# A four-layer graph network: attention sums in chunks of 32 edge tiles with a PSUM place for each tile, and four smaller edits

## The chip, the cores and the metric

The kernel runs on one core of one Trainium2 chip, in one launch. The metric is device time in microseconds (us), the median of several runs. A separate profiled execution gives the rows that are quoted here; it has its own time, which is given beside the median below. Engines are named as in the profile: PE (TensorE, with PEld for its weight loads), DVE (VectorE), ACT (ScalarE), POOL (GpSimd) and SP (SyncE), which here mostly issues DMAs.

## The reference

There are N = 6250 nodes with 128 features and E = 100000 edges sorted by their destination. The node features pass through four layers. After each of them stands `x = layernorm(x + layer(x))`.

- Layer 0 is graph attention, two sublayers: `g = h @ W`, one score per edge `e = leaky_relu(s[src] + d[dst])`, a softmax over the edges that share a destination, and `out = segment_sum(g[src] * alpha)`. A loop edge per node is included.
- Layer 1 is a graph convolution: `out = segment_sum(xw[row] * dis[row] * w * dis[col])`.
- Layer 2 is attention with eight heads. Per edge it has a relation embedding (64 types), a sigmoid time mask from `timestamps[dst] - edge_time`, a gate from a small network, then query of the destination, key and value of the message, softmax over the destination's edges, and a sum.
- Layer 3 sums `m[src]` over each destination's edges and feeds the sum to a GRU cell.

All of it is in float32. Each layer so has the same heart: rows of a node table are fetched for the sources of all edges, something is done per edge, and the results are summed per destination.

## The kernel before

**Edge tiles and blocks.** The nodes are 49 blocks of P = 128. The edges are packed into K = 832 tiles of 128 edges, each of which belongs to one block of destinations. A tile is summed by one matmul: its one-hot matrix `sel` (edge by node, f32, 128 x 128) is the stationary operand, the tile's 128 rows the moving one, and the product is what the tile adds to its block. `ACC` in SBUF holds the sums of all blocks, W = 136 columns each.

**Gathers.** `gather` (L137) is an indirect DMA on POOL's queue: 128 rows of a table in DRAM, one per partition. One stage has 832 of them. They fill row tiles `g` of U = 16 edge tiles.

**One-hot matrices.** `selections` (L365) gives `sel` for 16 tiles. In the first attention sublayer DVE makes it (L372) and SP stores it to `SELD`; later stages load it by SP (L370, 1 MB). `row_selections` (L377) gives the transposed one-hot `rsel` in bf16, which takes node values to edges. In the first sublayer it is made from a broadcast row of destination numbers (`dlrow`, L385) by a comparison on DVE (L386), and stored (L387); later it is loaded (L389).

**Sums.** The class `Windows` (L402) sums tiles in groups (L445) through a ring of PSUM banks. A bank is a window of 3 tiles (4 in `sum_edges`). The tiles of a window belong to neighbouring blocks, often to the same one, so a window has places for blocks relative to its first block: PE loads each tile's place into a register (L415, called in L434), the window is set to zero by a small matmul (L437, 1 x 128 by 1 x 408 or 512), and the tiles' matmuls accumulate at their places. DVE then adds the whole window to `ACC` (L453), at the register offset of the window's first block. Before the add of a chunk's first window, L451 fades what is in `ACC`, because the softmax reference of a block that goes on from the previous chunk may have changed.

**Attention.** `attention_edges` (L460) runs for l0 and l1. It takes the tiles in chunks, `CHUNKS = [48] * 17 + [16]`. Per chunk it loads flags (L483 on, SP), gathers the rows into `g` (7 buffers of 16 tiles), and forms the destination's value of each edge by small matmuls of `rsel` with values split into three bf16 terms (L493 into `pd`; in l0 also the node times, L496 into `pn`; the two lie in one bank, `pdn`). Then comes the softmax reference of the chunk, a chain between DVE and PE with transposes and scans (L499 to L547: `de`, `e`, `fw`, `tot`, `car`, `back`, `cin`, `ref`, `f`, `fac`). Then ACT takes the exponentials (L550) and scales each tile's rows (L556), and `sums.add` takes the tiles. The instructions of one chunk's sums and of the next chunk's chain stand between each other on the engines. The values for `rsel`'s matmuls come from `by_step` (L349), which makes one three-term table per value: `D0` for each sublayer, `NV` for the node times.

**The other edge stages.** `sum_edges` (L561) serves the graph convolution (c, with a scaling on ACT, L575) and the last layer (m, without): 8 buffers of `g`, windows of 4 tiles, two windows a group. Layer 2's table stage writes queries, `Qt`, split into three bf16 terms (L787 to L791). Its edge loop goes in 208 steps of B = 4 tiles: `rows_of` (L817) issues the gathers `xa`, the query loads `qb` (one per tile, at a register's offset, SP), the `rsel` loads and others; `keys` has for each tile one matmul for key and value (`pk`, L890) and three bf16 matmuls that bring the query to the edges (`pq`, L892). The values are stored to DRAM. The softmax reference (xw) follows, with flags loaded by SP (L1003), and then the sum (vw), which uses `Windows` with 3 tiles and 4 windows a group.

**What orders the work.** Within an engine instructions run in the order written out by the program's planner; across engines semaphores order them. `first_after(x, names)` (L392) makes `x` wait for the named instructions; `in_order` only keeps an order on one engine. A tile with n buffers makes its next use wait for the last reader n uses back: so POOL waits for PE, when it is as many row tiles ahead as there are buffers. DMAs of one engine's queue are issued in order.

Of the kernel before, what the change touches and what calls it, by code (L numbers as in the profile page):

```python
# [9 lines left out]
F32 = mybir.dt.float32  # L10
# [10 lines left out]
P = 128  # L21
NB = 49
# [17 lines left out]
CHUNKS = [48] * 17 + [16]  # L40
T = max(CHUNKS)
HD = 8
# [8 lines left out]
def kernel(ctx: ExitStack, tc: tile.TileContext, a: dict, out: bass.AP):  # L51
# [5 lines left out]
    def table(name, rows, width, dtype=F32):  # L57
        return dram.tile([rows, width], dtype, name=name)
# [20 lines left out]
    RSELD = table("rseld", K // U * P, U * P, BF16)  # L79
    TYR = table("tyr", KR, P, BF16)  # L80
# [5 lines left out]
    Qt = table("qt", NP, 3 * W, BF16)  # L86
# [30 lines left out]
    OFF = const.tile([97, K + 4], I32, name="OFF")  # L117
    PLACE = {3: OFF[0:1, 0:K], 4: OFF[64:65, 0:K]}
    QOFF = OFF[32:33, 0:K]
    FIRST = {3: OFF[96:97, 0:K // 3 + 1], 4: OFF[96:97, K // 3 + 1:K // 3 + 1 + K // 4]}  # L120
# [22 lines left out]
    with tc.tile_pool(name="prep", bufs=1) as pp, tc.tile_pool(name="prepp", bufs=2, space=PSUM) as pq:  # L143
# [97 lines left out]
        for m, w in WINDOWS.items():  # L241
            n = -(-K // m)
            part = 0 if m == 3 else 64
            steps = bkrow[part:part + 1, 0:n * m].rearrange("o (w s) -> o w s", s=m)
            place = pp.tile([P, K + 4], F32, name="place", bufs=2)[part:part + 1, 0:n * m]
            nc.vector.tensor_sub(place.rearrange("o (w s) -> o w s", s=m), steps,
                                 steps[:, :, 0:1].to_broadcast([1, n, m]))
            nc.vector.tensor_scalar(PLACE[m], place[:, 0:K], float(w), None, op0=OP.mult)
            nc.vector.tensor_scalar(FIRST[m], bkrow[96:97, 0:n * m:m], float(W), None, op0=OP.mult)
        nc.vector.tensor_scalar(QOFF, bkrow[32:33, 0:K], float(P), None, op0=OP.mult)  # L250

# [97 lines left out]
    def by_step(keep, work, psum, rows, name):  # L349


        v = work.tile([P, K], F32, name="bsv", bufs=1)
        for k0 in range(0, K, K // 2):
            pv = psum.tile([P, K // 2], F32, name="bs", bufs=1)
            nc.tensor.matmul(pv, rows, BSEL[0:NB, k0:k0 + K // 2], start=True, stop=True)
            nc.vector.tensor_copy(v[:, k0:k0 + K // 2], pv)
        t3 = keep.tile([P, K, 3], BF16, name=f"{name}t", bufs=1)
        for i in range(3):
            nc.vector.tensor_copy(t3[:, :, i], v)
            if i < 2:  # L360
                nc.vector.tensor_sub(v, v, t3[:, :, i])
        return t3
# [14 lines left out]
    def row_selections(work, k0, make=False, n=U):  # L377

        rs = work.tile([P, n * P], BF16, name="rsel", bufs=4 if n < U else 2)
        tab = RSELD[k0 // U * P:(k0 // U + 1) * P, k0 % U * P:(k0 % U + n) * P]  # L380
        if make:
            for h in range(2):
                n = U * P // 2
                row = work.tile([P, n], BF16, name="dlrow")
                nc.sync.dma_start(row, flat(DLR, k0 * P + h * n, (0, P), (1, n)))  # L385
                nc.vector.tensor_scalar(rs[:, h * n:(h + 1) * n], row, relid, None, op0=OP.is_equal)  # L386
            last = nc.sync.dma_start(tab, rs)  # L387
        else:
            last = nc.sync.dma_start(rs, tab)  # L389
        return rs, name_of(last)  # L390
# [10 lines left out]

    class Windows:  # L402
# [4 lines left out]
        def __init__(self, psum, m, banks, windows):  # L407
            self.m, self.w, self.banks, self.group = m, WINDOWS[m], banks, windows * m
            self.ring = psum.tile([P, banks, BANK], F32, name="ring")
            self.todo = []  # L410
            for t0 in range(0, NB + MW, 14):
                nc.vector.memset(ACC[:, t0:min(NB + MW, t0 + 14), :], 0.0)
# [7 lines left out]
        def add(self, k, sel, rows, after, fade=None, kept=0):  # L420

# [5 lines left out]
            if fade is not None:  # L427
                self.fades[k] = fade
# [18 lines left out]
            for v in wins:  # L447
                to = self.to[v % U]
                if v * m in self.fades:
                    a0 = ACCF[:, ds(to, kept)]  # L450
                    nc.vector.tensor_scalar(a0, a0, self.fades.pop(v * m), None, op0=OP.mult)  # L451
                a0 = ACCF[:, ds(to, m * W)].rearrange("p (b w) -> p b w", w=W)[:, :, 0:n]
                add = nc.vector.tensor_add(a0, a0, self.ring[:, v % self.banks, 0:m * w]  # L453
                                           .rearrange("p (b w) -> p b w", w=w)[:, :, 0:n])
                if v == wins[0]:
                    first_after(add, name_of(last))

        fades = {}

    def attention_edges(l, D3, NV3):  # L460
        extra = 1 if l == 0 else 0
        with ExitStack() as es:
            work = es.enter_context(tc.tile_pool(name=f"aw{l}", bufs=2))
            rows = es.enter_context(tc.tile_pool(name=f"ar{l}", bufs=7))
            psum = es.enter_context(tc.tile_pool(name=f"ap{l}", bufs=1, space=PSUM))
            sums = Windows(psum, 3, 6, 2)
# [6 lines left out]
            pd, pn = (pdn[:, i * 3 * T:(i + 1) * 3 * T].rearrange("p (t i) -> p t i", i=3) for i in range(2))  # L473
# [4 lines left out]
            for T_ in CHUNKS:  # L478
                gs = []
                flags = work.tile([T, 4, P], BF16, name="flags")[0:T_]  # L480
# [5 lines left out]
                for u0 in range(0, T_, U):  # L486
                    g = rows.tile([P, U, GW + 3], F32, name="g")
                    gs.append((g, [gather(g[:, q, 0:GW], Gt[l], SRCT[:, k0 + u0 + q:k0 + u0 + q + 1])
                                   for q in range(U)]))
                    rs, _ = row_selections(work, k0 + u0, l == 0)  # L490
                    for q in range(U):
                        k = k0 + u0 + q
                        nc.tensor.matmul(pd[:, u0 + q, :], rs[:, q * P:(q + 1) * P], D3[:, k, :],  # L493
                                         start=True, stop=True)
                        if l == 0:
                            nc.tensor.matmul(pn[:, u0 + q, :], rs[:, q * P:(q + 1) * P], NV3[:, k, :],  # L496
                                             start=True, stop=True)
                if l == 0:
                    nc.vector.tensor_reduce(TMT[:, k0:k0 + T_], pn[:, 0:T_, :], AX.X, OP.add)  # L499
                de = work.tile([P, T], F32, name="de")[:, 0:T_]  # L500
                nc.vector.tensor_reduce(de, pd[:, 0:T_, :], AX.X, OP.add)
# [59 lines left out]
    def sum_edges(name, src_tab, weighted):  # L561

        with ExitStack() as es:
# [3 lines left out]
            sums = Windows(psum, 4, 8, 2)  # L567
            for k0 in range(0, K, U):
                g = rows.tile([P, U, D], F32, name="g")
                got = [gather(g[:, q, :], src_tab, SRCT[:, k0 + q:k0 + q + 1]) for q in range(U)]  # L570
                sel, made_by = selections(work, k0)
                for q in range(U):
                    after = name_of(got[q])
                    if weighted:
                        scaled = nc.scalar.activation(g[:, q, :], g[:, q, :], AF.Copy,  # L575
                                                      scale=EWT[:, k0 + q:k0 + q + 1])
                        after += name_of(scaled)
                    sums.add(k0 + q, sel[:, q, :], g[:, q, :], made_by + after)

# [71 lines left out]
    with tc.tile_pool(name="l0", bufs=1) as lp:  # L651
        SD = [lp.tile([P, 2, NB], F32, name=f"SD{l}") for l in range(2)]
        D3 = [None, None]
        with tc.tile_pool(name="n0w", bufs=2) as work, tc.tile_pool(name="n0p", bufs=1, space=PSUM) as psum:
# [11 lines left out]
            NV3 = by_step(lp, work, psum, nv, "NV")  # L666
            D3[0] = by_step(lp, work, psum, node_rows(work, psum, SD[0][:, 1, :]), "D0")
        attention_edges(0, D3[0], NV3)
        with tc.tile_pool(name="n1w", bufs=2) as work, tc.tile_pool(name="n1p", bufs=1, space=PSUM) as psum:
# [6 lines left out]
            D3[1] = by_step(lp, work, psum, node_rows(work, psum, SD[1][:, 1, :]), "D0")  # L676
        attention_edges(1, D3[1], None)
# [47 lines left out]
    with tc.tile_pool(name="l2", bufs=1) as lp:  # L725
# [26 lines left out]
        with tc.tile_pool(name="n3w", bufs=2) as work, tc.tile_pool(name="n3p", bufs=1, space=PSUM) as psum:  # L752
# [21 lines left out]
            for t0, g in GROUPS:  # L774
# [5 lines left out]
                q3 = work.tile([P, B, 3, W], BF16, name="q3")  # L780
# [6 lines left out]
                for i in range(3):  # L787
                    nc.scalar.copy(q3[:, :g, i, :], qt[:, :g])
                    if i < 2:
                        nc.vector.tensor_sub(qt[:, :g], qt[:, :g], q3[:, :g, i, :])  # L790
                nc.sync.dma_start(nodes(Qt)[:, t0:t0 + g, :], q3[:, :g].rearrange("p t i w -> p t (i w)"))  # L791
# [5 lines left out]
        with ExitStack() as es0:  # L797
# [7 lines left out]
            with ExitStack() as es:  # L805
# [11 lines left out]
                def rows_of(n):  # L817
# [4 lines left out]
                    qb = rows.tile([P, B, 3, W], BF16, name="qb", bufs=4)  # L822
# [3 lines left out]
                    loads = [nc.sync.dma_start(qb[:, q].rearrange("p i w -> p (i w)"), Qt[ds(vals[q], P), :])  # L826
# [3 lines left out]
                    rs = row_selections(work, k0, n=B)  # L830
                    landed[n] = [i.ins.name for i in loads] + rs[1]
                    rs = rs[0]
# [45 lines left out]
                def keys(n, mT, qb, rs):  # L878
# [6 lines left out]
                    for q0 in range(0, B, 2):  # L885
                        pk = pks[:, q0 // 2]
                        pq_ = pqs[:, q0 // 2, 0:2 * W].rearrange("p (q w) -> p q w", w=W)
                        for q in range(q0, q0 + 2):
                            o = q * P
                            part(nc.tensor.matmul(pk[:, q - q0, :], mT[:, q, :], Wkv, start=True, stop=True), after)  # L890
                            for i in range(3):
                                part(nc.tensor.matmul(pq_[:, q - q0, :], rs[:, o:o + P], qb[:, q, i, :],  # L892
                                                      start=i == 0, stop=i == 2), after)
# [62 lines left out]
            with tc.tile_pool(name="xw", bufs=1) as work, tc.tile_pool(name="xp", bufs=1, space=PSUM) as psum:  # L956
# [40 lines left out]
                for g0 in range(0, NG, 4):  # L997
                    pr = psum.tile([P, 4, P], F32, name="prr", bufs=2)
                    for i in range(4):
                        tot = TOT[:, g0 + i, :]  # L1000
                        fl = work.tile([P, 2, P], BF16, name="fl", bufs=4)
                        for way in range(2):
                            flags_of(2 + way, fl[:, way, :], g0 + i, nc.sync)  # L1003
# [217 lines left out]
```

## Time and profile before

| | us |
|---|---|
| median of 3 runs | 8168.42 (8152.12 to 8171.95) |
| profiled execution, its time | 8259.27 |
| profiled execution, its span | 8257.5 |

The profiled span, by stage:

| stage | from | to | what |
|---|---|---|---|
| l0 | 146 | 1700 | attention, first sublayer |
| l1 | 1757 | 3213 | attention, second sublayer |
| c | 3345 | 4540 | weighted sum |
| tables | 4634 | 4687 | queries and other node tables of layer 2 |
| L2 loop | 4687 | 6410 | messages, keys, values, scores |
| xw | 6410 | 6512 | softmax reference of layer 2 |
| vw | 6512 | 6822 | sum of layer 2 |
| m | 6914 | 8133 | plain sum |

Over the span PE is busy 47%, DVE 32%, ACT 21%, POOL 51%. The profile's rows read as follows. In a row of the waits: engine, line and tile that waited, then the releaser, the sum in us, how often, and the longest. "issue" is time in which the engine waited for nothing that the profile shows, "remote" a releaser that it cannot name. In a row of the timeline: start and length in us, engine, line, operation, written tile and read tiles, shape, how many in a row, and in brackets the idle time before it with its releaser. The granted clock is TensorE's, as a share of full speed.

### The profile page before, as it was taken

To read this page: it belongs to the slowest core of one execution; us is meant where nothing else is said; L and a number is where in the kernel's file an instruction comes from. 1 tells how busy PE (TensorE), PEld (TensorE's weight loads), DVE (VectorE), ACT (ScalarE), POOL (GpSimd) and SP (SyncE) were. 2 spreads that over 40 slices of the span, in tenths; PEclk is the share of its full clock that TensorE was granted. 3 is DMA by queue.
4 is the path that set the end of the run, shared out by engine and by line. 5 is a ranking of instruction groups with operands and counts; after the bars stand their busy time and mean duration, and the time that the engine had idled before them with its cause. 6 is when DMAs were issued, how large, how long until landed. Compare 5 with 4: busy or idle time off the path is not lost. (4 is left out here: it accounts for less than half of the span.)

```text
span 8257.5 us, 75556 instructions
## 1 busy us (share of the span) xinstructions
PE 3922.3 (47%) x20491; PEld 2792.2 (34%) x20491; DVE 2618.2 (32%) x5807; ACT 1708.1 (21%) x5176; POOL 4221.7 (51%) x4384
## 2 busy tenths in 40 slices
PE   2244444433334433233333377777777693243436
PEld 1133333322223322222222244444444472132224
DVE  3122222231111114110111666566566654011115
ACT  1112121202211111222222233333333110000001
POOL 2555555435555551656666155455553373666661
PEclk8555555555555555555555688788888796555657
DMA  4333433333333322222332466666666592232321
GB/s 109 93 118 111 120 111 118 94 91 108 96 96 96 98 79 59 78 88 88 96 92 89 133 184 186 179 187 185 181 185 169 193 360 66 70 97 87 98 88 60
DMA packets 737110, 997.93 MB, mean 121 GB/s; under 512 B 151865, under 2 KB 594033, under 8 KB 703425
## 3 DMA queue, kind: packets, MB, share of 16 engines
q1 hardware_dynamic: 588090, 662.03, 25.4%
q0 software_dynamic: 146992, 331.03, 16.2%
q8 instruction: 189, 3.10, 0.2%
q14 instruction: 217, 1.77, 0.1%
q10 hardware_dynamic: 1622, 0.01, 0.0%
HBM read 824.55 MB, written 168.09 MB: 120 GB/s over the span
## 5 line engine op out<-in xcount | busy, mean ns | idle before, releaser
L445 PE MATMUL ring<-g,sel 128*128 128x128 f32 (+2 forms) x6656 | 1532.7, 388 | 1755.5 <-issue 1723.6
L137 POOL DMA_INDIRECT g<-g,SRCT x1664 | 1573.0, 945 | 1524.8 <-issue 836.9
L445 PEld LDWEIGHTS ring<-g,sel 128*128 128x128 f32 x6656 | 1336.8, 288 | 2119.7 <-issue 2119.6
L453 DVE TENSOR_TENSOR ACC<-ACC,ring 128x512 f32 (+3 forms) x1250 | 755.9, 605 | 3734.0 <-remote 2206.2
L137 POOL DMA_INDIRECT xa<-xat,SRCT x832 | 855.4, 1028 | 970.0 <-DVE z L872 582.5
L137 POOL DMA_INDIRECT g<-yt,SRCT x832 | 785.0, 943 | 589.8 <-issue 394.7
L137 POOL DMA_INDIRECT g<-mt,SRCT x832 | 785.0, 944 | 489.6 <-issue 345.5
L437 PE MATMUL ring<-zero 1*128 1x408 bf16 (+1 forms) x1250 | 446.5, 449 | 963.5 <-DVE ACC L453 564.6
L890 PE MATMUL pk<-Wkv,mT 128*128 128x256 f32 x1664 | 681.7, 499 | 94.2 <-DVE qk L900 49.0
L556 ACT ACTIVATE g<-g 128x128 f32<-128x128 f32 x1664 | 521.1, 388 | 186.1 <-issue 125.7
L575 ACT ACTIVATE g<-g,EWT 128x128 f32<-128x128 f32 x832 | 324.9, 400 | 863.9 <-DMA g<-yt,SRCT 767.6
L437 PEld LDWEIGHTS <-zero 1*128 1x128 bf16 x1250 | 106.9, 101 | 1073.6 <-issue 928.1
L890 PEld LDWEIGHTS pk<-Wkv,mT 128*128 128x128 f32 x1664 | 310.1, 232 | 132.2 <-DVE qk L900 62.1
L1027 POOL TENSOR_TENSOR vx<-v,exh 128x512 f32<-128x512 f32 x208 | 214.9, 1064 | 247.5 <-DMA v<-vt 221.2
L892 PE MATMUL pq<-qb,rsel 128*128 128x136 bf16 x2496 | 331.1, 250 | 0.0
L892 PEld LDWEIGHTS <-rsel 128*128 128x128 bf16 x2496 | 251.9, 114 | 177.6 <-issue 72.3
L898 ACT COPY kv<-pk 128x512 f32<-128x512 f32 x416 | 239.8, 600 | 348.1 <-PE pq L892 268.6
L542 ACT ACTIVATE f<-f 1x1 f32<-1x1 f32 x36 | 7.3, 202 | 1361.3 <-DVE f L541 1253.8
L860 PE MATMUL rp<-RT,oty 128*128 128x256 bf16 x832 | 259.8, 312 | 21.8 <-DMA qb<-qt 21.8
L323 ACT COPY aT<-tr 128x512 f32<-128x512 f32 (+1 forms) x13 | 7.3, 560 | 1232.2 <-PE tr L321 1232.2
L861 PE MATMUL rp<-RT,oty 64*128 64x256 bf16 x832 | 257.3, 309 | 0.0
L493 PE MATMUL pdn<-D0t,rsel 128*128 128x3 bf16 x1664 | 101.5, 167 | 321.6 <-issue 212.9
(322 smaller groups left out, 4531.4 us busy)
## 6 DMA issues: line engine op xcount, KB each, us to landing
sel<-seld SPq DMA_DIRECT2D x208, 1024.0 KB
qb<-qt SPq DMA_DIRECT2D x832, 102.0 KB
seld<-sel SPq DMA_DIRECT2D x52, 1024.0 KB
vt<-kv SPq DMA_DIRECT2D x208, 256.0 KB
v<-vt SPq DMA_DIRECT2D x208, 256.0 KB
g<-g,SRCT POOLq DMA_INDIRECT x1664
dlrow<-dlr SPq DMA_DIRECT2D x104, 256.0 KB
rseld<-rsel SPq DMA_DIRECT2D x52, 512.0 KB
```

The costliest lines, as they stand in the source:

```text
L137: return nc.gpsimd.indirect_dma_start(out=dst_tile, out_offset=None, in_=tab, in_offset=bass.IndirectOffsetOnAxis(ap=idx, axis=0))
L437: z = nc.tensor.matmul(self.ring[:, v % self.banks, 0:m * w], zero[:, 0:P], zero[:, 0:m * w], start=True, stop=False, skip_group_check=True)
L445: last = nc.tensor.matmul(self.ring[:, q // m % self.banks, ds(at[q - ks[0]], n)], sel, rows, start=False, stop=False, skip_group_check=True)
L453: add = nc.vector.tensor_add(a0, a0, self.ring[:, v % self.banks, 0:m * w] .rearrange("p (b w) -> p b w", w=w)[:, :, 0:n])
L556: scaled = nc.scalar.activation(g[:, q, 0:D], g[:, q, 0:D], AF.Copy, scale=g[:, q, D:D + 1])
L575: scaled = nc.scalar.activation(g[:, q, :], g[:, q, :], AF.Copy, scale=EWT[:, k0 + q:k0 + q + 1])
L860: part(nc.tensor.matmul(rp[:, q, :], oty[:, o:o + P], RT2, start=True, stop=False), after)
L861: part(nc.tensor.matmul(rp[:, q, :], oty[0:REL, o:o + P], RT3, start=False, stop=True), after)
L890: part(nc.tensor.matmul(pk[:, q - q0, :], mT[:, q, :], Wkv, start=True, stop=True), after)
L892: part(nc.tensor.matmul(pq_[:, q - q0, :], rs[:, o:o + P], qb[:, q, i, :], start=i == 0, stop=i == 2), after)
L898: free += [nc.scalar.copy(kv[:, q0:q0 + 2, :], pk), nc.scalar.copy(qbs[:, k0 % U + q0:k0 % U + q0 + 2, :], pq_[:, :, D:]), nc.vector.tenso ...
L1027: i0 = nc.gpsimd.tensor_mul(vx[:, :, 0:D].rearrange("p q (h d) -> p q h d", h=HD), v.rearrange("p q (h d) -> p q h d", h=HD), exh[:, u0:u0 ...
```

## The change

- Chunks are 32 tiles, `CHUNKS = [32] * 26`, with the same 7 row tiles.
- Attention sums by a new class, `Sums`. Its PSUM ring has 6 banks of 3 places, 18 in all, and each tile has a place of its own, at a fixed address. There is no zero matmul and no register load on PE. A group is 8 tiles. DVE adds each tile by itself, at the register offset of its block (`AOFF`, loaded 16 at a time). Layer 2's and `sum_edges`' sums keep `Windows`.
- Both node values stand in one table, `DN` (six terms a tile). In l0 one matmul brings both to the edges, and `pdn` is used by one chunk at a time; in l1 two chunks alternate in it. `rsel` has 3 buffers instead of 2.
- Layer 2's queries stay f32 (`Qt`, 136 columns), with no splitting. `sum_edges` for c also makes the transposed one-hot in f32 (`made_rows`) and stores it to `RSELF`; layer 2 loads that and has one f32 matmul for `pq` instead of three in bf16.
- In `sum_edges`, from the eighth row tile on, the first gather of every fourth row tile waits for the matmuls of the row tile five back.
- The second of the two flag loads at L1003 is issued by ACT.

```diff
-CHUNKS = [48] * 17 + [16]
+CHUNKS = [32] * 26
 T = max(CHUNKS)
+ROWS = 7
...
+    RSELF = table("rself", K // U * P, U * P)
...
-    Qt = table("qt", NP, 3 * W, BF16)
+    Qt = table("qt", NP, W)
...
+        nc.vector.tensor_scalar(AOFF, bkrow[0:1, 0:K], float(W), None, op0=OP.mult)
...
-    def row_selections(work, k0, make=False, n=U):
...
+    def row_selections(work, k0, make=False):
+
+        rs = work.tile([P, U * P], BF16, name="rsel", bufs=3)
...
+    def made_rows(work, k0, rs, tab):
+        for h in range(2):
+            n = U * P // 2
+            row = work.tile([P, n], BF16, name="dlrow")
+            nc.sync.dma_start(row, flat(DLR, k0 * P + h * n, (0, P), (1, n)))
+            nc.vector.tensor_scalar(rs[:, h * n:(h + 1) * n], row, relid, None, op0=OP.is_equal)
+        nc.sync.dma_start(tab, rs)
...
+    class Sums:
...
+        def add(self, k, sel, rows, after, fade=None, kept=0):
+
+
+            if k % U == 0:
+                _, self.to = nc.values_load_multi_w_load_instructions(
+                    AOFF[:, k:k + U], engines=[ET.DVE], min_val=0, max_val=(NB - 1) * W,
+                    skip_runtime_bounds_check_because="blocks are below NB")
+            if fade is not None:
+                self.fades[k] = (fade, kept)
+            self.todo.append((k, sel, rows, after, self.to[k % U]))
+            if k % self.group < self.group - 1 and k < K - 1:
+                return
+            todo, self.todo = self.todo, []
+            width = BANK // self.m
+            done = []
+            for q, sel, rows, _, to in todo:
+                n = rows.shape[-1]
+                at = self.ring[:, q // self.m % self.banks, q % self.m * width:q % self.m * width + n]
+                mm = nc.tensor.matmul(at, sel, rows, start=True, stop=True)
+                if not done:
+                    first_after(mm, [a_ for t in todo for a_ in t[3]])
+                else:
+                    in_order(mm, done[-1][0])
+                done.append((mm, q, at, n, to))
+            for mm, q, at, n, to in done:
+                if q in self.fades:
+                    fade, kept = self.fades.pop(q)
+                    a0 = ACCF[:, ds(to, kept)]
+                    nc.vector.tensor_scalar(a0, a0, fade, None, op0=OP.mult)
+                a0 = ACCF[:, ds(to, n)]
+                add = nc.vector.tensor_add(a0, a0, at)
+                if mm is done[0][0]:
+                    first_after(add, name_of(done[-1][0]))
...
-            sums = Windows(psum, 3, 6, 2)
+            sums = Sums(psum, 3, 6, 8)
+            nv = DN.shape[-1]
...
+                c0 = 0 if nv == 6 else k0 // T % 2 * T * nv
+                pd = pdn[:, c0:c0 + T * nv].rearrange("p (t i) -> p t i", i=nv)
...
-                        nc.tensor.matmul(pd[:, u0 + q, :], rs[:, q * P:(q + 1) * P], D3[:, k, :],
+
+                        nc.tensor.matmul(pd[:, u0 + q, :], rs[:, q * P:(q + 1) * P], DN[:, k0 + u0 + q, :],
                                          start=True, stop=True)
-                        if l == 0:
-                            nc.tensor.matmul(pn[:, u0 + q, :], rs[:, q * P:(q + 1) * P], NV3[:, k, :],
-                                             start=True, stop=True)
...
+                if len(ends) >= 8 and len(ends) % 4 == 0:
+
+                    first_after(got[0], ends[-5])
                 sel, made_by = selections(work, k0)
+                if weighted:
+                    made_rows(work, k0, work.tile([P, U * P], F32, name="rself", bufs=2),
+                              RSELF[k0 // U * P:(k0 // U + 1) * P, :])
...
-                for i in range(3):
-                    nc.scalar.copy(q3[:, :g, i, :], qt[:, :g])
-                    if i < 2:
-                        nc.vector.tensor_sub(qt[:, :g], qt[:, :g], q3[:, :g, i, :])
-                nc.sync.dma_start(nodes(Qt)[:, t0:t0 + g, :], q3[:, :g].rearrange("p t i w -> p t (i w)"))
+                nc.sync.dma_start(nodes(Qt)[:, t0:t0 + g, :], qt[:, :g])
...
-                            for i in range(3):
-                                part(nc.tensor.matmul(pq_[:, q - q0, :], rs[:, o:o + P], qb[:, q, i, :],
-                                                      start=i == 0, stop=i == 2), after)
+                            part(nc.tensor.matmul(pq_[:, q - q0, :], rs[:, o:o + P], qb[:, q, :],
+                                                  start=True, stop=True), after)
...
-                            flags_of(2 + way, fl[:, way, :], g0 + i, nc.sync)
+                            flags_of(2 + way, fl[:, way, :], g0 + i, (nc.sync, nc.scalar)[way])
```

## The prediction

> **What bounds the kernel now.** I read the busy shares by stage first, then what POOL, DVE and the `ring` tile wait for inside one stage, then one group of sums in order of time. The stages, from the windows view (start:end and length in us, then busy us and records of PE, PEld, DVE, ACT, POOL, then granted clock, DMA share, GB/s):
>
> ```profile
> 146.00:1700.00 1554.00, 615.75 (x3788) 472.71 (x3787) 388.26 (x841) 280.00 (x1000) 786.77 (x832) 0.54 0.36 107
> 1757.00:3213.00 1456.00, 535.15 (x2876) 402.88 (x2875) 213.42 (x646) 278.38 (x955) 785.71 (x832) 0.56 0.33 95
> 3345.00:4540.00 1195.00, 417.38 (x1673) 306.47 (x1674) 126.39 (x184) 324.88 (x832) 784.97 (x832) 0.57 0.29 88
> 4687.00:6410.00 1723.00, 1269.32 (x6687) 806.83 (x6687) 1016.53 (x2122) 633.57 (x1921) 854.85 (x832) 0.80 0.66 180
> 6914.00:8133.00 1219.00, 450.21 (x1872) 333.23 (x1872) 141.49 (x206) 0.00 (x0) 785.04 (x832) 0.59 0.30 90
> ```
>
> They are l0 and l1 (attention), c (weighted sum), the edge loop of layer 2, and m (plain sum). Four of them are 832 gathers each. A gather takes 0.944 us and the next starts 0.30 us later, so POOL needs 832 x 1.2475 = 1038 us if it never pauses. c and m take 1.15 to 1.17 times that, l1 1.40, l0 1.50. No engine is full in l0 and l1: they stand in a chain. POOL's waits in l1, and DVE's:
>
> ```profile
> POOL g L137 <- issue: 591.7, 824, 30.0
> DVE de L503 <- DMA g<-g,SRCT: 277.2, 24, 15.3
> DVE ACC L453 <- PE ring L445: 273.2, 67, 6.5
> DVE ACC L453 <- remote: 233.5, 26, 21.1
> DVE ACC L453 <- PE pch L516: 168.1, 9, 20.7
> ```
>
> POOL's 591.7 less 832 x 0.30 leaves about 342 us of pauses, some 15.6 + 7.9 us per chunk, when it is seven row tiles (112 edge tiles) ahead and the next buffer is still read by PE. DVE meanwhile waits 277 us for gathers of the chunk that POOL could not start. So each side waits for the other: a chunk of 48 holds three row tiles in the sums and three in the softmax, and one of seven is left as lead. Inside the sums the groups run one behind the other:
>
> ```profile
> 2614.76 1.16 DVE L453 TENSOR_TENSOR ACC<-ACC,ring 128x390 f32 x2 [1.32 <-remote]
> 2615.97 0.83 PE L437 MATMUL ring<-zero 1*128 1x408 bf16 x2 [12.13 <-DVE ACC L453]
> ...
> 2617.64 2.96 PE L445 MATMUL ring<-g,sel 128*128 128x130 f32 x12 [0.84 <-issue]
> ...
> 2620.64 1.16 DVE L453 TENSOR_TENSOR ACC<-ACC,ring 128x390 f32 x2 [4.73 <-PE ring L445]
> ...
> 2621.86 0.83 PE L437 MATMUL ring<-zero 1*128 1x408 bf16 x2 [1.25 <-DVE ACC L453]
> ```
>
> Six tiles take 5.9 us (zeros 0.83, the load of places 0.84, matmuls 2.96, adds 1.16, gaps), though other banks of the ring are free. Over a chunk, 8 x 5.9 = 47 us of about 83; the rest are the waits for gathers and a stretch in which PE's instructions start 2 to 3 us apart with nothing to wait for ("issue").
>
> **The change, part by part.** *Attention.* Removed per layer: 278 zero matmuls (266 recorded x 0.49 = 130 us of PE) and 139 place loads (0.84 us or more each, 117 us at least). The tile's matmuls go to fixed places, 18 of them, in groups of 8: 2.96 / 6 x 8 = 3.95 us a group. The next group takes other places, so it need not wait for the adds. Added: one add per tile. The add takes 0.561 us for 390 columns and 0.687 for 512 (c), which is 1.03 ns a column, so 131 columns 0.294 us: 832 x 0.294 = 245 us against 264 x 0.561 = 148, **+97 us of DVE**, and 52 loads of 16 places instead of 18, +34 x 1.1 = 37 us. DVE is busy 213 of l1's 1456 us, so both fit, behind PE's next matmuls. [...] I take nothing, and keep 194 for the case that the adds come to stand on the chain.
>
> What sets the end instead? A chunk of 32 holds two row tiles in the sums and two in the softmax: three of seven are POOL's lead. Its least is 32 x 1.2475 = 39.9 us a chunk, its most, if nothing is won, 83 x 32 / 48 = 55.3. The nearest row is c, with the same gathers and f32 matmuls: POOL's long pauses there (3.99 us before 3776.07, 6.14 us before 3821.85) come every 45.8 us, for 32 tiles. The softmax chain per chunk (26 instead of 18 chains, DVE some 5.4 us busy each) runs between groups, as now. **I take 46.5 us in l1.** In l0, where DVE also makes the two kinds of one-hot (388 us busy before), 48. One matmul for both node values takes 832 small matmuls from l0 (167 ns each, 26 ns apart in a run): below 30 us of PE and hidden in 48.
> l1: 26 x 46.5 + 17 for start and tail (1456 less 17.33 x 83) = 1226, **-230**. l0: 26 x 48 + 80 (1554 less 17.33 x 85) = 1328, **-226**.
>
> [...] I keep 0.49 us a tile. [...]
>
> *c.* One-hot rows in f32 are made and stored: 104 loads of 256 KB and 52 stores of 1 MB, in SP's queue behind and ahead of the `sel` loads, and 104 comparisons on DVE (about 1.1 us each, from `sel`'s 2048 columns in 2.285 us). DVE is 126 of 1195 us busy and the DMA share 0.29 (some 81 MB more on 105 MB), so they hide. If not, the comparison waits behind the adds, the store behind it, the next `sel` behind the store, and PE behind `sel`: 52 x 2 us = +100. Between 0 and 100, near the first by these shares: **+10**.
>
> *Row tiles four at a time (c, m).* POOL waits once in 64 tiles until PE is at most 64 behind. PE then holds 64 x 1.43 = 92 us of gathered work, so a longer pause of POOL starves nobody. No row shows it; -20 to +40 a stage, taken as **0**, since PE's own pace sets the end.
>
> *Layer 2.* Three bf16 matmuls (59 ns apart) become one f32 of 136 columns: by `pk`, 484 ns for 256 columns in full flow, 257 ns against 177, 832 x 80 = +66 us if PE is the bound. PE is busy 1269 of 1723 us and the loop also waits for DVE and `qb`; the query loads shrink from 102 to 68 KB while the row one-hots double to 256 KB, about even. Ends -20 and +130 (at a lower clock); half of 66: **+35**. Before the loop 39 casts and 26 subtractions go (23.6 + 17.9 us, partly side by side), and POOL's first gather waits for this stretch: **-10**. Half the flag loads of the later layer-2 stage go to ACT's queue: at most 10 us, taken as 0.
>
> Sum: -230 - 226 + 10 + 35 - 10 = -421. From the profiled 8259.3 (span 8257.5): 7838. The median of the runs stands at 8168.4 / 8259.3 = 0.989 of it: **7752, say 7750**.
>
> **Rivals.** *The chain keeps its length* (slower). From the first transpose of a softmax to its last step (2558.6 to 2597.5 in l1) are 39 us, each step queued behind a group of sums or a slow stretch of PE. If that is a price per chunk, not per tile, then 39 + 12 of gather wait + 4 groups of 3.95 = 67 us a chunk: l1 26 x 67 + 17 = 1759 (+303), l0 +268, in all 606 more with layer 2, 8770. It decides from 55.3 us a chunk. For it: 26 chains, and the slow stretch has no cause in the profile. Against it: half of the 39 us are groups of the chunk before, and the gather waits come from lead that now grows.
> *Half a gain*: slow issue on PE stays once per chunk, 51 us in l1 and 52.5 in l0: -113 - 109 + 35 = 7980.
> *POOL never pauses*: 39.9 us, l1 -401, l0 -436, +35: 7370. Against it: c, which has no softmax, still pauses.
> *It does not do what it says*: groups still wait for the adds before, because what orders them isn't the ring's window reads; 55 us a chunk, l0 and l1 as now, layer 2 decides: 8170 to 8230.
>
> **How the numbers follow.** As c: 0.52. Half: 0.15. No pauses: 0.12. No effect: 0.05 (of it 0.03 within 0.3%, about what a measurement tells from no change, 0.02 beyond). Longer chain: 0.16. Faster 0.79, same 0.03, slower 0.18. The likeliest alone is 7600 to 7900 (cycles of 43 to 50 us, layer 2 from -20 to +130). The range leaves out the slower cases and the end of no pauses: **7480 to 8150**.
>
> **What would show it.** Right: l1's chunks 44 to 49 us apart; POOL's pauses in l0 and l1 below 200 us; `de` waits for gathers under 100 us; matmuls of the next group start before the adds of the last end; DVE about 320 us busy in l1. Layer 2's loop 1700 to 1790 us, c and m within 40 us. Wrong: chunks at 55 us or more with the softmax steps far apart, adds waited for by PE, or PE's 2 to 3 us starts filling each chunk; in c, `sel` late behind the stores.

## The result, and the profile after

The changed kernel takes 8176.03 us (median of 12 runs, 8163.13 to 8194.58) against 8168.51 (12 runs) for the kernel before: ratio **1.0013, 95% interval 1.0003 to 1.0022**. That is no gain where 7750 us were forecast. The profiled execution has a span of 8174.9 us. The median of the kernel before varied by session: 8168 to 8272 us in four of six, 7024 and 7031 in two. Every comparison of medians below is made within one session, unless the text says otherwise.

The stages in the windows view of the changed kernel, in the order l0, l1, c, loop of layer 2, m, with the columns as in the prediction:

```profile
143.00:1507.00 1364.00, 460.63 (x2758) 414.06 (x2757) 480.75 (x1542) 273.71 (x1008) 792.70 (x832) 0.57 0.41 121
1562.00:3079.00 1517.00, 462.17 (x2758) 413.02 (x2758) 319.92 (x1354) 267.33 (x963) 790.86 (x832) 0.53 0.32 91
3184.00:4501.00 1317.00, 435.54 (x1872) 324.48 (x1872) 206.84 (x307) 319.27 (x832) 796.44 (x832) 0.58 0.46 145
4606.00:6250.00 1644.00, 1286.62 (x5867) 940.08 (x5867) 1038.21 (x2121) 629.48 (x1921) 856.54 (x832) 0.82 0.68 186
6757.00:8052.00 1295.00, 419.88 (x1872) 305.74 (x1872) 142.07 (x207) 0.00 (x0) 786.62 (x832) 0.58 0.28 85
```

l0 is 190 us shorter, and layer 2's loop 85 when it is taken to its last matmul. l1 is longer by some 30 us by the same count. (The rows of before in the prediction's windows were cut some 30 us before that in l1 and in c, and 10 in layer 2's loop.) c is 93 longer by the same count and m 75. Together with the small stages this makes 83 us less for this pair of profiles. The medians say 7.5 more: that profile of before stood 90 us above its median, and this one stands at its own. So the signs are read from the profiles, and the sizes of the parts, further down, from medians.

**What m shows.** In m the wait for four row tiles is the only edit. The first gather after a pause of POOL, in the timeline of the kernel before:

```profile
7183.26 0.95 POOL L137 DMA_INDIRECT g<-mt,SRCT  x1 [5.88 <-PE ring L445]
```

and in that of the changed kernel:

```profile
7239.75 0.94 POOL L140 DMA_INDIRECT g<-mt,SRCT  x1 [20.53 <-PE ring L495]
```

Before, POOL stops for 5.9 us after 32 gathers; now for 18 to 21 us after 64. PE in the changed kernel around this pause, which lasts from 7219.2 to 7239.75:

```profile
7226.48 0.55 PE L495 MATMUL ring<-g,sel 128*128 128x128 f32 x1 [0.36 <-issue]
7229.26 1.03 PE L495 MATMUL ring<-g,sel 128*128 128x128 f32 x4 [2.22 <-issue]
...
7231.18 3.78 PE L495 MATMUL ring<-g,sel 128*128 128x128 f32 x16
...
7242.45 2.05 PE L495 MATMUL ring<-g,sel 128*128 128x128 f32 x16
...
7254.57 0.39 PE L495 MATMUL ring<-g,sel 128*128 128x128 f32 x1
7256.67 0.37 PE L495 MATMUL ring<-g,sel 128*128 128x128 f32 x1 [1.71 <-issue]
7258.77 0.37 PE L495 MATMUL ring<-g,sel 128*128 128x128 f32 x1 [1.73 <-issue]
```

A group of 8 tiles (16 records) goes in 2 to 4 us from ten microseconds after POOL stopped until about eleven after it went on. Outside that, PE starts its instructions at multiples of 0.70 us, with "issue" before them, and a group takes 33 to 44 us. So **PE is slow while POOL issues gathers**, and it stays slow for a while after POOL stops. (That the gathers are the cause is shown only by the experiments that space them.) The lag, from the end of POOL's last gather to the first point where twelve records of PE, weight loads and waits counted, start within 2.2 us, in c and m of both kernels:

| gathers in POOL's run | 160 | 128 | 64 | 32 | 16 |
|---|---|---|---|---|---|
| lag, us | 24.0, 22.5 | 17.4, 17.5 | 7.5 to 10.1 | 2.7 to 5.5, mostly 4.0 to 4.2 | 1.9 to 3.5 |

That is about 0.14 us per gather. I read it as a backlog: as if each gather left some 1.39 us of work somewhere (an estimate, 1.2475 and 0.14) while POOL issues one each 1.2475. The profile does not show where.

**What l1 shows.** From about 2120 to 2815 us, POOL in l1 is in a cycle of 58.0 us for 32 tiles. One such chunk in the timeline:

```profile
2547.57 0.99 PE L541 MATMUL pdn<-DN,rsel 128*128 128x3 bf16 x32
2548.63 0.23 PE L561 MATMUL pch<-ident,tot 32*1 32x32 f32 x1
2564.06 0.95 POOL L140 DMA_INDIRECT g<-g,SRCT  x1 [0.31 <-issue]
2569.57 0.32 SPq L386 DMA_DIRECT2D rsel<-rseld  x1
2570.45 0.27 DVE L564 TENSOR_TENSOR_SCAN car<-scf,car,pch 1x32 f32<-1x32 f32 x1 [21.73 <-remote]
2583.31 0.95 POOL L140 DMA_INDIRECT g<-g,SRCT  x1 [18.30 <-issue]
```

PE's transposes are recorded at 2548.6. DVE, which waits for PE's semaphore, goes on at 2570.45, and SP's load, which waits for the small matmuls, at 2569.57: 5.4 and 4.6 us after POOL's last gather ended (2565.0). So what PE reports is held up too, by these records, and two engines that wait for different matmuls of PE see it within 0.9 us of each other. The chain then finishes and frees row tiles, POOL runs for 32 gathers, and the next chain stands again. The waits of DVE and PE in l1 carry it:

```profile
DVE car L564 <- remote: 375.7, 19, 21.7
...
DVE de L548 <- DMA g<-g,SRCT: 131.2, 18, 13.4
PE pch L570 <- DVE back L568: 361.3, 19, 22.2
PE ring L440 <- DVE ACC L452: 182.0, 68, 14.8
```

The last line is a second surprise. The groups of sums still run one behind the other:

```profile
2462.74 3.84 PE L440 MATMUL ring<-g,sel 128*128 128x130 f32 x16 [1.82 <-DVE ACC L452]
2466.61 2.56 DVE L452 TENSOR_TENSOR ACC<-ACC,ring 128x130 f32 x8 [3.66 <-PE ring L440]
2469.23 3.83 PE L440 MATMUL ring<-g,sel 128*128 128x130 f32 x16 [2.66 <-DVE ACC L452]
```

6.5 us for 8 tiles (0.81 a tile) instead of 5.9 for 6 (0.98). The zeros and the loads of places are gone, the wait for the adds is not. The second group here is number 54 of the stage, counted from 0; its places in the ring begin at 8 x 54 = 432, which is 0 modulo 18, so at the start of a bank.

### The profile page after: what moved, and what is told of

Read it like the earlier page. It is cut to its first block, busy times and chain, and to the rows that moved or that the text cites. A ratio compares the mean times of both kernels' runs of the same rounds, so it can differ in the third digit from the quotient of the medians.

```text
span 8174.9 us, 72553 instructions
## 1 busy us (share of the span) xinstructions
PE 3648.8 (45%) x18431; PEld 2832.7 (35%) x18431; DVE 2886.9 (35%) x7290; ACT 1658.6 (20%) x5153; POOL 4247.0 (52%) x4384
## 4 chain that ended last, share of the span: by engine, by line
issue 24%; PE 18%; POOL 17%; DVE 8%; another core or an unknown queue 8%; DMA 5%; ACT 4%; DVEq 0%; SPq 0%; ACTq 0%; POOLq 0%
POOL g L140 15%; PE ring L495 4%; PE pk L939 4%; PE ring L440 3%; POOL xa L140 2%; PE pq L940 2%; DMA v<-vt 1%; ACT g L601 1%; DVE ACC L452 1%; PE ring L487 1%; DMA g<-yt,SRCT 1%; ACT kv L946 1%; PE rp L910 1%; PE rp L909 1%
## 5 line engine op out<-in xcount | busy, mean ns | idle before, releaser
L495 PE MATMUL ring<-g,sel 128*128 128x128 f32 x3328 | 708.1, 344 | 1527.7 <-issue 1479.3
L500 DVE TENSOR_TENSOR ACC<-ACC,ring 128x512 f32 (+1 forms) x694 | 446.1, 643 | 2289.1 <-remote 1555.8
L440 PE MATMUL ring<-g,sel 128*128 128x131 f32 (+1 forms) x3328 | 776.7, 425 | 617.1 <-DVE ACC L452 373.9
L452 DVE TENSOR_TENSOR ACC<-ACC,ring 128x131 f32 (+1 forms) x1664 | 475.7, 286 | 1062.3 <-remote 598.1
L940 PEld LDWEIGHTS pq<-qb,rsel 128*128 128x128 f32 x1664 | 409.0, 246 | 84.6
L940 PE MATMUL pq<-qb,rsel 128*128 128x136 f32 x1664 | 406.7, 334 | 0.0
L939 PEld LDWEIGHTS pk<-Wkv,mT 128*128 128x128 f32 x1664 | 337.0, 248 | 182.9 <-DVE qk L948 153.0
L487 PE MATMUL ring<-zero 1*128 1x512 bf16 (+1 forms) x694 | 227.2, 416 | 273.6 <-issue 131.9
L948 DVE TENSOR_TENSOR qk<-kv,pq 128x256 f32<-128x256 f32 x416 | 173.7, 418 | 283.4 <-ACT qbs L947 155.0
```

What stands on the lines that cost most here:

```text
L440: mm = nc.tensor.matmul(at, sel, rows, start=True, stop=True)
L452: add = nc.vector.tensor_add(a0, a0, at)
L487: z = nc.tensor.matmul(self.ring[:, v % self.banks, 0:m * w], zero[:, 0:P], zero[:, 0:m * w], start=True, stop=False, skip_group_check=True)
L495: last = nc.tensor.matmul(self.ring[:, q // m % self.banks, ds(at[q - ks[0]], n)], sel, rows, start=False, stop=False, skip_group_check=True)
```

## The experiments

Two theories. **Backlog**: POOL's gathers, closer together than about 1.39 us, put PE into the slow pace; the wait for four row tiles makes POOL's runs longer, and so the pauses; l1 stands for the same reason. **Rivals**: the wait costs nothing and c and m suffer from the added transfers; or the slow pace belongs to the profiler.

### The wait for four row tiles, alone and left out

Left out of the changed kernel:

```diff
-                if len(ends) >= 8 and len(ends) % 4 == 0:
-
-                    first_after(got[0], ends[-5])
```

and the same lines alone added to the kernel before.

> The changed kernel without the wait for four row tiles in c and m. Backlog theory (while POOL issues gathers without a pause, PE falls into a slow pace and stays in it for about 0.14 us per gather of the run after POOL has stopped: 24.0, 17.4, 10.0 and 4.1 us after runs of 160, 128, 64 and 32 gathers): the wait makes runs of 64, whose pauses of 18.7 us replace two of 5.9, so m goes back from 1295 to 1219 us and c from 1317 to about 1240, and the whole from 8176 to about 8025. Rival (c and m are longer for the added transfers, or the slow pace is of the profile only): 8176 within 20.

> The kernel before with the wait for four row tiles alone. Backlog theory: m 1295, c about 1270 to 1295 us, the whole from 8168 to about 8310. Rival (the wait costs nothing): 8168 within 20.

Both fell into a session where the kernel before takes 7024.28 us. Left out: 6994.17, ratio 0.9952 (0.9935 to 0.9969). Alone: 7026.19, ratio 1.0003 (0.9994 to 1.0012). Neither number can tell the theories apart, since here PE has no slow stretch at all. The stages l0, l1, c, loop of layer 2 and m of the kernel before with the wait, in that session:

```profile
146.00:1268.00 1122.00, 581.01 (x3788) 453.02 (x3786) 389.16 (x842) 271.44 (x1000) 790.35 (x832) 0.56 0.48 148
1324.00:2558.00 1234.00, 546.04 (x2956) 415.20 (x2954) 221.89 (x660) 263.83 (x955) 786.27 (x832) 0.56 0.36 112
2660.00:3707.00 1047.00, 487.75 (x1872) 373.19 (x1872) 141.75 (x207) 318.51 (x832) 785.29 (x832) 0.59 0.32 105
3827.00:5357.00 1530.00, 1234.58 (x6706) 788.00 (x6707) 1021.39 (x2125) 640.77 (x1923) 859.97 (x832) 0.84 0.72 203
5857.00:6903.00 1046.00, 489.31 (x1872) 373.99 (x1872) 141.44 (x206) 0.00 (x0) 785.07 (x832) 0.58 0.32 105
```

c and m are POOL's 832 x 1.2475 = 1038 us and little more: this is the kernel without the slow pace. l0 stands 84 us above that floor, l1 196. The same program runs with the slow pace in one session and without it in another, so the program alone does not bring it about. Nor does the chip alone: the one that the record numbers 13 gave the kernel before 7024 us here and 8265 beside the last run below. The granted clock does not tell the two apart either (here 0.56 to 0.59 in l0, l1, c and m; in the result 0.53 to 0.58). Since the medians without profile differ by as much, it is not the profiler's. What differs between the sessions is not known.

Both were run again.

> The changed kernel without the wait for four row tiles, on the chip of the changed kernel itself. Where the slow pace occurs the wait costs two pauses of 5.9 against one of 18.7 us per 64 tiles: m 1219, c 1240, the whole 150 us below the changed kernel. Where it doesn't occur POOL never pauses and the wait costs nothing: within 10 us.

> The kernel before with the wait for four row tiles alone, once more. Where PE falls into the slow pace, by the difference that leaving it out of the changed kernel made (8186 less 7992): +170 to +195, about 8360, c 1315 and m 1294. Rival: in the kernel before it costs nothing, 8176. Where PE keeps its pace: nothing, as measured before (7026 beside 7024). Its profile also shows l0, l1 and layer 2 of the kernel before a second time.

These fell into sessions with the slow pace. Left out: **7991.62** beside the changed kernel's 8186.01 and the kernel before's 8176.02 in that session, ratio 0.9771 (0.9736 to 0.9807): 194 us less than with the wait, of which the profiles show 106 in c (1331 to 1225) and 84 in m (1294 to 1210). Alone: 8472.95 beside 8272.27, ratio 1.0242 (1.0216 to 1.0267), 200 us more. So the wait costs all that the rest of the change gains, and c's added stores and comparisons cost little: with them, but without the wait, c takes 1225 us, and 1223 in the profile of before (1061 beside 1046 where there is no slow pace).

### The attention part, and the change itself again

The attention part is the changed kernel with `Qt`, `pq`, `sum_edges` and the flag loads as before; then the flag loads on ACT's queue were added to it.

> The kernel before with the attention part alone (chunks of 32, a place for each tile, both node values in one matmul). By the two profiles l0 takes 1364 us against 1554 and l1 1517 against 1456: about 8168 - 130 = 8040. If the profile of the kernel before stands 90 us above its median because of l0 or l1, it is 8130. By the prediction as it was on record: 7720.

> The changed kernel itself, beside the kernel before on the same chip. Theory: whether PE falls into the slow pace during POOL's gathers is a condition of the chip in that session, not of the kernel. Where it doesn't occur (before near 7024), the change gives 6994 to 7000, ratio 0.996; where it does (before near 8168), 1.001 as in the result. Rival: the ratio does not depend on it: 1.001 in both.

> The attention part and the flag loads on ACT's queue; bf16 queries and no wait for four row tiles. From the attention part alone (6935 us beside 7024) less 17 us of the stage of layer 2's reference (97 against 80): 6918, ratio 0.985, where PE keeps its pace. Where PE falls into the slow pace, about 8168 - 160 - 17 = 7990, ratio 0.98.

Without the slow pace the attention part alone takes 6935.04 beside 7024.28, ratio 0.9876 (0.9859 to 0.9892): l1 goes from 1234 (in the profile above) to 1125 us, and l0 stays where it was, 1122 and 1124. With the f32 queries and the flags of the first experiment it is 6994, so these cost 59 us net. Layer 2's loop takes 1604 us there instead of 1525, of which the table stage gives back 16 and the reference stage 17; c takes 15 more.

With the slow pace the changed kernel gave 8186.01 beside 8176.02, ratio 1.0007 (0.9995 to 1.0019), the result again. Attention and flags gave 8034.73, ratio 0.9821 (0.9793 to 0.9850). The medians beside these divide the change: attention and flags **-141**, f32 queries with all they need -43 (7992 against 8035), the wait **+194**, together +10. (7990 was expected for attention and flags.) The expectation that the ratio depends on the session was not tested for the whole change, which has no run in a session without the slow pace. The wait alone bears it out: 1.0003 without, 1.0242 with.

### Spacing the gathers

If the gathers are too close together, spacing them must help PE, though it slows POOL. After each gather of l0, l1, c and m POOL clears a small tile, from one column up; the wait for four row tiles is left out:

```diff
-    def gather(dst_tile, tab, idx):
...
+    def gather(dst_tile, tab, idx, pace=False):
...
+        if pace:
...
+            for _ in range(2):
+                paced.append(nc.gpsimd.memset(spare, 0.0))
+                in_order(paced[-1], got)
```

> The changed kernel without the wait for four row tiles, and with one small POOL memset after each gather of l0, l1, c and m, so that a gather takes some 1.40 to 1.50 us instead of 1.2475. Backlog theory: at 1.39 us and more nothing piles up, PE has no slow stretches, c and m take 832 x the new pace + 40 (1205 to 1290 us), l1's chain is not held up and falls from 1517 to 1230 to 1320, l0 to 1280 to 1370: the whole 7750 to 7950. Rival (POOL's pace only adds to the stages): 4 x 832 x 0.2 = 660 us more than without the memset, 8690.

> The changed kernel without the wait for four row tiles, with two POOL memsets of 160 columns after each gather of l0, l1, c and m (one of one column vanished in the 0.30 us between gathers). A gather then takes some 1.4 to 1.6 us. Where PE keeps its pace, POOL is the bound and c and m grow from 1046 to 832 x the new pace + 10, 1175 to 1340. Backlog theory, where the slow pace occurs: nothing piles up at 1.39 us and more, and they take the same 1175 to 1340 with no stretch of PE at 0.70 us, l1 the same instead of 1517. Rival there: the pace adds to the pauses, c and m 1340 to 1500.

One column once: 6974.48 beside 7024.28, ratio 0.9927 (0.9910 to 0.9943), with no change of POOL's pace, as the 0.12 us fit into the 0.30 between two gathers. It told nothing about the backlog. Two of 160 columns made a gather each 1.64 us, in a session with the slow pace: 8410.55, ratio 1.0284 (1.0246 to 1.0321). That is longer, as it must be at this pace (832 x 1.64 = 1364 us a stage). c and m took 1426 and 1395 us, which by itself fits the rival. But l1 became shorter, 1506 to 1426 us, and PE's unnamed waits ("issue") in c and m are 6 and 0.4 us, where the same kernel without memsets has 686 and 674. So a pace between 1.39 and 1.64 should beat both kernels.

> The changed kernel without the wait for four row tiles, with two POOL memsets of 56 columns after each gather of l0, l1, c and m: by the rows of the run before (0.95 us of gather, 0.27 us for 160 columns, 0.12 for one, 0.15 between) a gather every 1.42 to 1.45 us, just above the 1.39 at which the backlog was read to begin. Backlog theory, where PE falls into the slow pace: no such stretch is left; c and m 832 x 1.43 + 15 = 1205, l1 1250 to 1290 instead of 1506, l0 1270 to 1310 instead of 1373: the whole about 7650, well below both kernels. Rival (the bound lies higher, between 1.43 and 1.64 us, or pauses and pace add): slow stretches stay and the time is that of the same kernel without memsets, 7990, or more. Where the slow pace doesn't occur: 832 x 0.18 x 4 = 600 us more than the 6994 without the memsets.

> The kernel before with the same two memsets of 56 columns. Backlog theory, where the slow pace occurs: c and m 1205; l0 and l1 lose their slow stretches and the waits behind them, to 1300 or so each, about 7720. If the serial sums and the chunks of 48 are what bounds l0 and l1, they stay at 1450 and more, about 8080. Where it doesn't occur, 600 us more than 7024.

Two of 56 columns gave 1.462 us per gather. The timeline of POOL in the changed kernel so spaced:

```profile
7000.49 0.95 POOL L143 DMA_INDIRECT g<-mt,SRCT  x1
7001.44 0.36 POOL L149 MEMSET spare<- 128x56 f32 x2
7001.95 0.95 POOL L143 DMA_INDIRECT g<-mt,SRCT  x1
```

**7826.02 beside 8272.27, ratio 0.9461 (0.9444 to 0.9478).** Its l0, l1, c and m:

```profile
144.00:1476.00 1332.00, 456.21 (x2758) 408.99 (x2757) 478.77 (x1541) 271.40 (x1008) 1059.35 (x2496) 0.56 0.43 124
1534.00:2821.00 1287.00, 459.79 (x2758) 412.38 (x2757) 322.90 (x1351) 263.67 (x963) 1046.19 (x2496) 0.55 0.38 108
2925.00:4203.00 1278.00, 486.96 (x1872) 373.17 (x1872) 211.23 (x310) 320.22 (x832) 1071.19 (x2496) 0.56 0.46 150
6450.00:7701.00 1251.00, 486.60 (x1872) 372.13 (x1872) 141.96 (x207) 0.00 (x0) 1041.40 (x2496) 0.58 0.29 88
```

and what PE waits for in m, first in the kernel before, then in the changed kernel so spaced:

```profile
PE ring L445 <- issue: 692.6, 378, 4.5
...
PE ring L501 <- DMA g<-mt,SRCT: 766.7, 104, 15.7
PE ring L509 <- issue: 0.3, 1, 0.3
```

In m PE now waits for its data, and for nothing unnamed. l1 falls from 1506 us, in another session with the slow pace, to 1287, with slower gathers. c and m pay some 50 and 40 us for the wider pace. The whole was expected near 7650; 832 x 4 x 0.03 = 100 us of the miss are the wider pace, the rest was not looked into. The kernel before with the same memsets: 7953.57, ratio 0.9616 (0.9598 to 0.9635), with l0 1329 and l1 1316 us (7720 was expected, with c and m at 1205; they took 1253 and 1251). So it was not the serial sums and the chunks of 48 that held l0 and l1 at 1490 to 1560, but mostly what the spacing took away, PE's slow pace and its late reports. With the spacing the change without the wait is worth 128 us, of which 29 lie in l1, none in l0 and most in layer 2.

> As the run with 56 columns (a gather every 1.462 us, 7826 us beside 8272), but two memsets of 30 columns: about 1.40 us, at the edge of the 1.39 that the lags after POOL's runs gave. Backlog theory with that size: still no stretch of PE at 0.70 us, l0, l1, c and m each 832 x 0.06 = 50 us shorter, ratio to the kernel before 0.92 to 0.935. Rival (the true edge lies between 1.40 and 1.46): the stretches are back, l1 near 1500, ratio 0.96 to 0.98. Where PE keeps its pace in the kernel before too: 832 x 0.15 x 4 = 500 us more than without memsets, ratio 1.07.

> The kernel with two memsets of 30 columns once more (a gather about every 1.40 us), for a session in which PE falls into the slow pace. Backlog theory with the size 1.39: no stretch at 0.70 us is left, ratio to the kernel before 0.92 to 0.935. Rival (the edge lies between 1.40 and 1.46): the stretches are back, l1 near 1500, ratio 0.96 to 0.98. Where PE keeps its pace: 1.087, as measured.

Two of 30 columns gave 1.42 us per gather. The first of these runs fell into a session without the slow pace: 7641.03 beside 7030.66, ratio 1.0866 (1.0848 to 1.0884). The spaced kernel is 610 us longer where spacing isn't needed. The second, with the slow pace: **7759.86 beside 8265.15, ratio 0.9387 (0.9371 to 0.9404)**, the fastest kernel of the sessions with the slow pace, and just outside the 0.92 to 0.935 of the backlog theory. The two runs are one kernel without and with the slow pace, and their stages show what is left of it at 1.42 us: c takes 1243 us in both, m 1217 and 1219, l0 1295 and 1301, but l1 1251 and 1309. There DVE's `car` again waits for an unnamed releaser, 20 times and 211 us in all; at 1.462 us it did so twice, for 19 us. So in l1 the edge lies between 1.42 and 1.46 us, a little above the 1.39 from the lags.

Two things the spacing does not separate. It also spaces the gathers' transfers, so whether POOL's instructions or the traffic that they start hold PE up is open. And a memset that leaves POOL's pace as it is ran only where PE had no slow stretch, so that the memsets work by their length, and not by being there, rests on 30 columns leaving part of the delay in l1 and 56 columns almost none.

## Why the prediction was wrong

The failed steps, by the profiles: of the forecast -421 came -83. Of the 338 us between them l1 makes 260, c and m 158 and l0 36, and layer 2's loop takes 120 off. The factor 0.989 added 86 to the miss.

**l0 held in its number**: -226 forecast, -175 to -190 in the profiles. The reason given is not borne out: where the slow pace is absent (1122 and 1124 us) or the gathers are spaced (1329 and 1332) the change gains nothing in l0, though POOL's own pace may hide a gain there. By my count of PE starts at multiples of 0.70 us, five or more in a row, l0 had 214 us of them before and has none after, about what was gained. Why the changed kernel escapes them there is not shown, so this is in part luck.

**l1 failed, and cost most, at the step "The nearest row is c ... I take 46.5 us in l1"**. The cycle became 58.0 us, and the stage 1517 us where 1226 were forecast. c's row was the same pace of POOL but not the same kind of dependence: in c nothing waits for PE's report within a group, in l1 a chain of five exchanges with PE does, and the one that falls into POOL's run waits until about 5 us after its end. That POOL's pace is the cause is shown by the spacing, which brings l1 to 1287 us. The slower rival had named the place ("each step queued behind a group of sums or a slow stretch of PE") and the point from which it decides, 55.3 us. Its price was too high (67 us a chunk), since one step waits, not all of them, and it does not hold in l0 (1364 / 26 = 52 us). Without the slow pace the attention part gives 109 us in l1 and nothing in l0, against 230 and 226, since POOL's floor is near.

**The wait for four row tiles was the second error**: "a longer pause of POOL starves nobody ... since PE's own pace sets the end", taken as 0, within -20 to +40 a stage. For c and m together it cost 194 us in the changed kernel and 200 in the kernel before. PE's pace was not its own: it followed POOL's runs. The rows to see it were in the trace of before, where "issue" is 704 of PE's 780 us of waits in c, 735 of 771 in m and half of them in l0 and l1, but 64 of 461 in layer 2's loop. I had noted that as a stretch "with nothing to wait for" and kept it as a rival, when its end just after POOL stops would have shown the tie.

**"The next group takes other places, so it need not wait for the adds"** failed: it waits (182 us, 68 times in l1). A bank in common is not the reason. Every third group begins at the start of a bank, in which the group before has no place, and in l1 and l0 these too start no earlier than 0.05 us after the last add of the group before, as in the rows above. What makes them wait stays open. So a group costs 6.5 us, not 3.95. DVE's added adds were near the size given: 0.29 us each, 320 us busy in l1. They stand on the chain between groups, the case for which the prediction kept 194 us (twice its 97, for two sublayers), so their time need not be hidden; what they cost was not separated.

**The clock** stayed at 0.53 to 0.58 in l0, l1, c and m, where it was 0.54 to 0.59 before, and the 0.49 us a tile that the prediction kept held (3.84 us for 8 tiles in l1, as in the rows above). In l1 PE waits 2.66 us between groups, so they did not come back to back. Where they do, in m's pauses of POOL, a group's matmuls go from 3.78 to 2.05 us and the granted clock from 0.50 to 1.00. The 1.00 came 10 us after the dense work began in the pause shown, and 4 us after it in a pause of the kernel before; what sets that time is not shown.

**Layer 2**: +35 forecast, within -20 to +130. Without the slow pace +74 to +79, near the +66 of the step for a loop bound by PE, though PE's busy time grew by 51 only (1235 to 1285). In the result's profiles it is -85, outside the ends. This loop, whose gathers no edit spaces, feels those sessions too: in the kernel before, with the wait or the memsets added, it takes 1530 us without the slow pace and 1731 to 1738 with it; with f32 queries 1604, and 1638 to 1646. That turns the sign; why the f32 loop loses less is not shown. Attention and flags, with bf16 queries, show 1673 us for this loop against some 1730, so only 29 of the 85 go with the queries; the other 56 stay unexplained. The flags on ACT's queue gave 17 us, not 0, and the tables 12 to 18, not 10. vw, which no step named, became 18 to 26 us longer in most variants, the kernel before with memsets among them; it was not looked into.

**The factor 0.989** from profile to median was taken as fixed, but it was this one profile's excess: the profile of the changed kernel stands at its median.

## What to carry to other kernels

Read an idle engine's "issue" rows against what the other engines do at the same time. Where a slow stretch ends just after another engine stops, try the length of that engine's runs as a cause. A producer that runs ahead isn't free: here, in sessions with the slow pace, longer runs and rarer pauses of the gathering engine cost 200 us, and slowing it by 17% made the kernel before 4% faster. Measure such a remedy in more than one session, because where the slow pace did not occur a spaced kernel was 9% slower.

## What the runs showed that I had not expected

- While POOL issues an indirect gather each 1.25 us, PE can issue at multiples of 0.70 us, and engines that wait for it go on up to 21 us late. The lag after a run grows by about 0.14 us a gather. At 1.46 us a gather almost none of it is left in l0, l1, c and m. What the two engines share is open.
- It occurs in some sessions only, on one chip in one session and not in another. Where it occurs, the kernel before takes 8168 to 8272 us instead of 7024 to 7031.
- A POOL memset of one column (0.12 us) between two gathers costs no time: it fits into the 0.30 us between them.
